# Layer 0 of a two-layer graph network on one core: products ahead of their sums, turned rows copied behind the products, columns read one iteration later

## The chip, the cores and the metric

The kernel runs on one core of a Trainium2 chip. A core has five engines that run side by side, each through its own list of instructions in order: TensorE (PE, matrix products, with a weight load PEld that overlaps them), VectorE (DVE), ScalarE (ACT), GpSimd (POOL) and SyncE (SP). They wait for each other on semaphores only. SP, ACT and POOL also start transfers (DMA), which 16 DMA engines carry out. The metric is the device time of one execution in microseconds (us); less is better. The kernel before takes 928.87 us, the median of 6 runs that lie between 926.46 and 931.57.

## The reference, cut to what matters

`x` has 3327 rows of 512 numbers, `adj` is a 0/1 matrix of 3327 x 3327, symmetric, with ones on its diagonal and about nine ones in a row. Layer 0 is graph attention with 4 heads of 128 numbers, then relu, the addition of the input and a normalisation of each row:

```python
feats = jnp.einsum('nf,hfo->hno', X, W)
e_s = jnp.einsum('hno,ho->hn', feats, a_self)
e_n = jnp.einsum('hno,ho->hn', feats, a_neigh)
logits = e_s[:, :, None] + e_n[:, None, :]
logits = jnp.where(logits > 0, logits, LRELU_ALPHA * logits)
logits = logits + NEG_INF * (1.0 - A)[None, :, :]
attn = jax.nn.softmax(logits, axis=-1)
out = jnp.einsum('hnm,hmo->hno', attn, feats) + b[:, None, :]
...
x = _layernorm(x + relu(out))
```

Layer 1 weighs the neighbours' new rows in a second way, adds a plain sum over neighbours, two gates, two projections and a second normalisation. It is not touched by the change, apart from its line numbers.

## The kernel before

**Sparse lists.** The kernel does not multiply by `adj`. A first stage (to about 207 us of the span) turns the matrix into a short list of neighbours for each row, computes `feats` and the two scores for all rows, and writes them as rows of 520 numbers to a table in device memory (`table0`). Rows are sorted by their number of neighbours into 26 tiles of 128 rows. `CAPS[j]` is the number of neighbours that tile j has room for (14 down to 5 in the first group of 12 tiles, 14 down to 4 in the second group of 14). The first tile of each group has a "stair" more, one slot in which longer lists share rows. The first group's sorted lists come through device memory; the second group's are sorted in place by `sort1` (two of its 14 tiles in each of the iterations 1 to 7), which lets TensorE place rows by a 0/1 matrix and ends with two VectorE copies out of PSUM into `srt[1]`. `climb` then works out the node ids of a stair (`ids2`).

**The stage in question** is the loop over `order0`, the 26 tiles of layer 0, from about 207 to 531 us of the span. For each tile:

- *Gather.* POOL issues one indirect transfer for each slot (`indirect`, L615): 128 rows of the table, picked by a column of the list, into a ring of 42 slots (`ring`). The first one of a tile brings two slots, the tile's own x and its own features. `plan` lays out all slots beforehand; `gather` issues what fits in the program's order. A gather into a slot waits, by semaphore, for the instructions that read the slot's former content, above all for the TensorE product 42 slots earlier. POOL has 254 gathers in layer 0, in order, and nothing between them; after the last one come 14 scatters (`put_rows`, L146), which write the second group's finished rows to `table1`.
- *Weights.* `weigh_a` and `weigh_b`: some eight short VectorE instructions and one ScalarE exponential give the attention weights of a tile. They read every slot of the tile, so they wait for its last gather. ScalarE also copies ids and the tile's own x out of the ring (L768, L771).
- *Sum.* `attend`: each slot's 512 numbers are multiplied by the weights, on VectorE (L797) or, for every third slot, on ScalarE in four pieces (L795). TensorE adds the slots up in PSUM by products with the identity (L803), one fp32 product being two matmul instructions. `attend` issues the products and sums of a tile slot by slot and, behind slot 2, calls `between`, which is `columns2` of the tile two places earlier. `lean` tiles add the bias on VectorE (L802) to slot 0 instead of by a product of their own (L789).
- *Finish.* `finish` (L885, VectorE: relu and the addition of x) waits for the sum; `norm.add` takes statistics and, at the ends of groups of 4, 4, 4, 4, 4, 3, 2 and 1 tiles, a reciprocal square root in 13 short instructions.
- *Columns.* The new row is needed in 8 small products for layer 1. `columns1` turns the row on TensorE (L822), `columns2a` copies it out of PSUM on ScalarE (L828), `columns2` multiplies (L834), `columns3` copies the 8 results on VectorE (L838).
- *Publish.* `publish` normalises a group's tiles (L842 on ScalarE, L845 and L846 on VectorE) and starts the write to `table1`, two iterations after the group's end.

Nothing reorders instructions: each engine works through them as the Python code issues them. Before, one iteration i of the loop issues in this order: publish; `columns2a` of tile i-2; `attend` of tile i with `columns2` of tile i-2 inside; `finish` of tile i-1 and further gathers; `columns1` and statistics of tile i-1; `columns3` of tile i-2; `sort1`; `climb` at i = 8; `weigh` of tile i+1. Tiles 0 and 1 are attended ahead of the loop. Places (0 to 25) are counted along `order0`.

Layer 1 gathers from `table1` through the same ring, so its first gather waits for the last write of layer 0.

Of the kernel before, what the change touches and what calls it, by code (L numbers as in the profile page):

```python
# [78 lines left out]
def sparse_pass(  # L79
# [463 lines left out]
    def sort1(to, t0, t1):  # L543


        n = NG[1]
        if t0 == 0:
            in_place.append(ps.tile([P, KT * P], F32, tag="pt", name="sorted1")[:, : n * W1])
        for t in range(t0, t1):
            row_is = ls.tile([P, P], F32, tag="row_is", name=f"row_is{t}", bufs=2)  # L550
            nc.vector.tensor_scalar(row_is, columns, to[:, 1, t : t + 1], None, ALU.is_equal)
            spread = ls.tile([P, n, W1], F32, tag="spread", name=f"spread{t}", bufs=2)
            nc.vector.scalar_tensor_tensor(
                spread, tiles_.to_broadcast([P, n, W1]), to[:, 0, t : t + 1],
                st1[:, t : t + 1, :].to_broadcast([P, n, W1]), ALU.is_equal, ALU.mult,
            )
            nc.tensor.matmul(
                in_place[0], row_is, spread.rearrange("p t w -> p (t w)"), start=(t == 0), stop=(t == n - 1)
            )
        if t1 == n:  # L560
            by_tile = in_place[0].rearrange("p (t w) -> p t w", t=n)
            nc.vector.tensor_copy(srt[1][:, :, : S + 2], by_tile[:, :, : S + 2])
            nc.vector.tensor_copy(srt[1][:, :, S + 2 : W1].bitcast(F32), by_tile[:, :, S + 2 :])
# [34 lines left out]
    def climb(g, pool, psum):  # L598

        of = pool.tile([P, B + H], F32, tag="of", name=f"of{g}")  # L600
        nc.vector.tensor_copy(of[:, :B], srt[g][:, 0, C0 + 1 : S + 1])
        nc.vector.tensor_copy(of[:, B:], srt[g][:, 0, S + 2 : S + 2 + H].bitcast(F32))
        nc.tensor.matmul(psum, to_row, of, start=True, stop=True)
        nc.vector.tensor_mul(of[:, :B], psum[:, :B], step_of)
        id_ = pool.tile([P, 1], F32, tag="id_", name=f"id_{g}")
        nc.vector.tensor_reduce(id_, of[:, :B], AX.X, ALU.add)
        nc.vector.tensor_copy(ids2[g], id_)
        nc.vector.tensor_copy(es2[g], psum[:, B:])
# [134 lines left out]
    def weigh_a(j):  # L743
# [6 lines left out]
        if j in T0:  # L750
            logit = m0.tile([P, H], F32, tag="logit", name=f"logit{j}")
            nc.vector.tensor_add(logit, stair[j][:, F : F + H], es2[g])
            small = psx.tile([P, B * H], F32, tag="pcol", name=f"to_nodes{j}", bufs=2)
# [19 lines left out]
    def weigh_b(j):  # L773
# [5 lines left out]
        if j in T0:  # L779
            small = psx.tile([P, B * H], F32, tag="pcol", name=f"to_rows{j}", bufs=2)  # L780
            ws2[j] = to_rows(m0, small, f"n{j}", w[:, C0 + 1 :, :])

    def attend(j, lean, between):


        w = ws[j]
        acc = accs[j] = ps.tile([P, F], F32, tag="acc", name=f"acc{j}", bufs=2)
        if not lean:
            nc.tensor.matmul(acc, ident, bias0, start=True, stop=False)  # L789
        for s0, n, buf, o in got[j]:  # L790
            for s in range(s0, s0 + n):
                gv = buf[:, o + s - s0, 0:F].rearrange("p (h o) -> p h o", h=H)
# [7 lines left out]
                row = buf[:, o + s - s0, 0:F]  # L800
                if lean and s == 0:
                    nc.vector.tensor_add(row, row, bias0)  # L802
                nc.tensor.matmul(  # L803
                    acc, ident, row, start=(lean and s == 0), stop=(s == CAPS[j] and j not in T0)
                )
                if s == 2:
                    between()
        if j in T0:
# [4 lines left out]
            nc.tensor.matmul(acc, to_node, stair[j][:, 0:F], start=False, stop=True)  # L813

# [76 lines left out]
    for i in range(len(chunks)):  # L893
# [13 lines left out]
        if i == NC0 + 2:  # L907
            climb(0, p0, psl.tile([P, CH], F32, tag="pc1", name="climb0")[:, : B + H])
# [29 lines left out]
    for j in order0[:2]:  # L938
        weigh_a(j)
        weigh_b(j)  # L940
    for j in order0[:2]:
        attend(j, False, lambda: None)
    weigh_a(order0[2])
    weigh_b(order0[2])
    for j in order0[:2]:
        finish(j)
    ready = [[], []]
    for i in range(NT + 3):
# [3 lines left out]
        third = order0[i - 2] if 2 <= i < NT + 2 else None  # L952
        if third is not None:
            columns2a(third)
        if 2 <= i < NT:
            attend(order0[i], i >= 3, lambda: third is None or columns2(third))
        elif third is not None:
            columns2(third)
        if 0 < i <= NT:
            j = order0[i - 1]  # L960
            y = row1(j)[:, 0:F]
            if i > 2:
                finish(j)
            if not waiting:
                put_rows()
            columns1(j)
            done = norm.add(i - 1, y)
            if done:
                k0, scale, shift = done
                ready[1] = [  # L970
                    (order0[k], scale[:, k - k0 : k - k0 + 1], shift[:, k - k0 : k - k0 + 1]) for k in range(k0, i)
                ]
        if i > NT:
            put_rows()
        if 2 <= i < NT + 2:
            columns3(order0[i - 2])
        if 0 < i <= 7:
            sort1(rankis[1], 2 * i - 2, 2 * i)
        if i == 8:
            climb(1, m0, psx.tile([P, B * H], F32, tag="pcol", name="climb1", bufs=2)[:, : B + H])  # L980
# [10 lines left out]
        if 2 <= i < NT - 1:  # L991
            weigh_a(order0[i + 1])
            weigh_b(order0[i + 1])
# [658 lines left out]
```

## Time and profile before

One execution was profiled. It took 932.01 us, of which its span on the core is 930.1 us; 1.9 us lie around the span. It is 3.1 us above the median of the 6 runs.

| stretch of the span, us | PE busy, us | DVE busy, us | ACT busy, us | POOL busy, us |
|---|---|---|---|---|
| 207 to 245 (38) | 29.14 | 24.80 | 13.99 | 29.74 |
| 245 to 290 (45) | 45.00 | 35.04 | 17.95 | 34.64 |
| 290 to 340 (50) | 41.72 | 34.61 | 20.82 | 38.11 |
| 340 to 390 (50) | 43.90 | 42.45 | 24.39 | 38.42 |
| 390 to 440 (50) | 48.34 | 39.84 | 26.38 | 37.12 |
| 440 to 490 (50) | 48.80 | 41.44 | 26.19 | 37.99 |
| 490 to 530 (40) | 33.16 | 32.68 | 17.97 | 25.23 |

How to read it: busy time is the time in which an engine executes. The short step between two instructions in which it takes up the next one is not counted, nor is a wait. Matmul ends are modelled, so a PE that is busy throughout need not be at its peak. On the timeline of one engine each line has the start, the duration, the instruction with what it writes and reads, how often it is repeated, and in brackets the idle time before it with the event that ended it.

### The profile page before, as it was taken

What the parts mean: (1) busy time and instruction counts of PE and PEld (TensorE: products, weight loads), DVE (VectorE), ACT (ScalarE), POOL (GpSimd) and SP (SyncE); (2) the same over time, 40 slices, a digit from 0 to 9 for tenths busy, and PEclk for the clock granted to TensorE, in tenths of its full rate; (3) what the DMA queues carried; (4) which work ended last, traced back from release to release, by engine and by line L of the source; (5) the groups of instructions that cost most, each with busy time, mean ns of one, the idle gap of its engine ahead of it and who ended that gap; (6) DMA issues with size and microseconds to landing.
All of it is one profiled execution on the core that took longest, in us unless ns stands there. A gap on an engine that the chain in (4) does not pass through costs nothing. (4 is left out here: it accounts for less than half of the span.)

```text
span 930.1 us, 10307 instructions
## 1 busy us (share of the span) xinstructions
PE 784.7 (84%) x2518; PEld 413.7 (44%) x2518; DVE 734.5 (79%) x2100; ACT 288.1 (31%) x820; POOL 604.0 (65%) x641
## 2 busy tenths in 40 slices
PE   4698987327999889799998749999989999999893
PEld 3476775112455444344444414444444444444341
DVE  4387888884978668869887748799989989999973
ACT  0121221003355434445554312323231232322331
POOL 6710152757877777777777477777777777777611
PEclk9898998557899989799999859999999999999997
DMA  9999899999678788797777367777777777776401
GB/s 334 370 380 394 339 340 383 381 360 412 202 228 267 233 233 266 233 347 232 218 233 229 126 188 192 199 193 191 193 193 191 186 195 192 195 190 193 156 35 38
DMA packets 73349, 224.68 MB, mean 242 GB/s; under 512 B 12736, under 2 KB 16784, under 8 KB 72384
## 3 DMA queue, kind: packets, MB, share of 16 engines
q0 software_dynamic: 46368, 153.69, 55.4%
q1 hardware_dynamic: 24256, 68.13, 19.4%
q10 hardware_dynamic: 2656, 2.10, 0.7%
q8 instruction: 23, 0.38, 0.2%
q14 instruction: 46, 0.38, 0.1%
HBM read 203.02 MB, written 31.51 MB: 252 GB/s over the span
## 5 line engine op out<-in xcount | busy, mean ns | idle before, releaser
L615 POOL DMA_INDIRECT ring<-table,srt x464 | 485.0, 1045 | 158.7 <-issue 56.4
L803 PE MATMUL acc<-ring,ident 128*128 128x512 f32 x504 | 241.1, 623 | 21.7 <-DVE ring L802 15.0
L1097 DVE SCALAR_TENSOR_TENSOR sw<-ring,e,sw 128x512 f32<-128x512 f32 x226 | 169.3, 749 | 11.7 <-ACT sw L1081 7.5
L803 PEld LDWEIGHTS acc<-ring,ident 128*128 128x128 f32 x504 | 95.2, 198 | 134.2 <-issue 75.1
L1118 PE MATMUL acc<-ring,ident 128*128 128x512 f32 x264 | 126.6, 609 | 19.3 <-DMA ring<-table,srt 9.7
L371 PE MATMUL pf<-w,xc 128*128 128x260 f32 x416 | 105.0, 416 | 13.3 <-DVE w L311 13.3
L797 DVE TENSOR_TENSOR ring<-ring,w 128x512 f32<-128x512 f32 x176 | 111.8, 693 | 0.6
L371 PEld LDWEIGHTS pf<-w,xc 128*128 128x128 f32 x416 | 85.6, 208 | 30.1 <-DVE w L311 14.0
L1137 PE MATMUL po<-wsa,sT 128*128 128x512 f32 x208 | 95.0, 600 | 0.3 <-ACT sT L1130 0.3
L1137 PE MATMUL po<-wg,sT 128*128 128x512 f32 x208 | 93.7, 593 | 0.0
L795 ACT ACTIVATE ring<-ring,w 128x128 f32<-128x128 f32 x304 | 91.5, 390 | 0.0
L1118 PEld LDWEIGHTS acc<-ring,ident 128*128 128x128 f32 x264 | 49.9, 194 | 89.7 <-issue 45.4
L383 POOL DMA_DIRECT2D table<-row x26 | 14.3, 549 | 84.0 <-ACT st L380 81.6
L1099 DVE TENSOR_TENSOR ring<-ring 128x512 f32<-128x512 f32 x94 | 65.0, 692 | 3.2
L1169 ACT ACTIVATE za<-za 128x512 f32<-128x512 f32 x26 | 16.4, 632 | 151.5 <-DVE za L1167 151.5
L1137 PEld LDWEIGHTS po<-wsa,sT 128*128 128x128 f32 x208 | 40.2, 194 | 51.2 <-issue 48.7
L1137 PEld LDWEIGHTS po<-wg,sT 128*128 128x128 f32 x208 | 39.4, 190 | 48.8 <-issue 47.8
L402 PE MATMUL pc<-at,pow 128*32 128x512 bf16 (+1 forms) x182 | 23.5, 414 | 34.2 <-DMA at<-in_adjB 23.5
L762 ACT ACTIVATE w<-w 128x40 f32<-128x40 f32 (+10 forms) x26 | 6.2, 238 | 131.9 <-DVE w L761 131.9
L375 ACT COPY row<-pf 128x512 f32<-128x512 f32 x26 | 15.2, 586 | 97.0 <-PE pf L371 51.4
L1130 ACT COPY sT<-pt 128x512 f32<-128x512 f32 x52 | 28.4, 587 | 39.0 <-PE pt L1128 39.0
L834 PEld LDWEIGHTS pcol<-v,xt 128*128 128x128 f32 x208 | 28.8, 202 | 14.6 <-issue 12.2
(254 smaller groups left out, 938.3 us busy)
## 6 DMA issues: line engine op xcount, KB each, us to landing
at<-in_adjB SPq DMA_DIRECT2D x78, 512.0 KB, 11.6
ring<-table,srt POOLq DMA_INDIRECT x464, 3.9
table<-row POOLq DMA_DIRECT2D x26, 260.0 KB, 6.1
xc<-in_xB SPq DMA_DIRECT2D x6, 1024.0 KB, 8.6
own<-in_xo SPq DMA_DIRECT2D x1, 3640.0 KB, 45.2
own<-table SPq DMA_DIRECT2D x1, 3640.0 KB, 55.3
at<-in_adjL SPq DMA_DIRECT2D x13, 256.0 KB, 10.5
table<-in_xo SPq DMA_DIRECT2D x1, 3120.0 KB, 28.9
```

What stands on the lines that cost most here:

```text
L371: nc.tensor.matmul(pf[:, hh, :HC], xc[:, k, o : o + P], w0[:, k, hh, :], start=(k == 0), stop=(k == KT - 1))
L402: nc.tensor.matmul(pc[32 * c : 32 * c + 32, : nt * P], pow2[:, s, :], loaded[i, m], start=(s == 0), stop=(m + 1 not in ms or s == 3),)
L615: return nc.gpsimd.indirect_dma_start(out=out_, out_offset=None, in_=table, in_offset=bass.IndirectOffsetOnAxis(ap=ap, axis=0)).ins
L795: nc.scalar.activation(gv[:, h, :], gv[:, h, :], AF.Copy, scale=w[:, s, h : h + 1])
L797: nc.vector.tensor_tensor(gv, gv, w[:, s, :].rearrange("p (h o) -> p h o", o=1).to_broadcast([P, H, FO]), ALU.mult)
L803: nc.tensor.matmul(acc, ident, row, start=(lean and s == 0), stop=(s == CAPS[j] and j not in T0))
L834: nc.tensor.matmul(pcol, xt1[:, k, :], v1[:, k, :], start=(k == 0), stop=(k == KT - 1))
L1097: nc.vector.scalar_tensor_tensor(sw, g[:, i, 0:F], e[:, s : s + 1], sw, ALU.mult, ALU.add)
L1099: nc.vector.tensor_add(g[:, i, 0:F], g[:, i - 1, 0:F], g[:, i, 0:F])
L1118: nc.tensor.matmul(plain[j], to, row, start=(not sums_of_two and i == 0), stop=(sums_of_two and i == len(rows) - 1),)
L1130: nc.scalar.copy(sT, pt)
L1137: nc.tensor.matmul(proj[j], sT[:, k, :], wt[:, k, :], start=(half + k == 0), stop=(half + k == KT))
```

## The change

The function `attend` is split in two. `multiply` issues all multiplications of a tile (the same instructions on VectorE and ScalarE), `add_up` then all its TensorE sums; the call in the middle is gone. `climb` and the end of `sort1` are split off (`climb_a`, `climb_b`, `sorted1`). The loop starts at tile 0 with only `weigh` of tile 0 ahead of it, has one iteration more at its end, and issues in another order:

```diff
-    norm = Norm(...)
-    for j in order0[:2]:
-        weigh_a(j)
-        weigh_b(j)
-    for j in order0[:2]:
-        attend(j, False, lambda: None)
-    weigh_a(order0[2])
-    weigh_b(order0[2])
-    for j in order0[:2]:
-        finish(j)
+    weigh(at_(0))
     ready = [[], []]
-    for i in range(NT + 3):
-        for args in ready[0]:
-            publish(*args)
-        ready = [ready[1], []]
-        third = order0[i - 2] if 2 <= i < NT + 2 else None
-        if third is not None:
-            columns2a(third)
-        if 2 <= i < NT:
-            attend(order0[i], i >= 3, lambda: third is None or columns2(third))
...
+    for i in range(NT + 4):
+        cur, nxt, done, turned_ = at_(i), at_(i + 1), at_(i - 1), at_(i - 2)
+        past = [at_(k) for k in ([i - 3] if i < NT else [i - 2]) if at_(k) is not None]
+        if i == NT:
+            past = [at_(i - 3)] + past
+        if cur is not None:
+            multiply(cur, i >= 3)
+        if cur is not None:
+            add_up(cur, i >= 3)
+        if done is not None:
+            finish(done)
+            columns1(done)
+            if not waiting:
+                put_rows()
+            norm_done = norm.add(i - 1, row1(done)[:, 0:F])
+        if nxt is not None:
+            weigh(nxt)
+        if turned_ is not None:
+            columns2a(turned_)
+            columns2(turned_)
+        for j in past:
+            columns3(j)
+        for args in ready[0]:
+            publish(*args)
+        ready = [ready[1], []]
+        if i > NT:
+            put_rows()
...
+        if i < 7:
+            sort1(rankis[1], 2 * i, 2 * i + 2)
+        if i == 7:
+            sorted1()
         if i == 8:
-            climb(1, m0, ...)
+            climb_a(1, m0)
+        if i == 9:
+            climb_b(1, m0)
...
-        if 2 <= i < NT - 1:
-            weigh_a(order0[i + 1])
-            weigh_b(order0[i + 1])
```

The new function for the sums:

```diff
+    def add_up(j, lean):
+
+        acc = accs[j] = ps.tile([P, F], F32, tag="acc", name=f"acc{j}", bufs=2)
+        rows = [] if lean else [(ident, bias0)]
+        rows += [(ident, buf[:, o + k, 0:F]) for _, n, buf, o in got[j] for k in range(n)]
+        if j in T0:
+            rows.append((to_node, stair[j][:, 0:F]))
+        for k, (to, row) in enumerate(rows):
+            nc.tensor.matmul(acc, to, row, start=(k == 0), stop=(k == len(rows) - 1))
```

So, within an iteration: ScalarE multiplies tile i before it copies turned rows, and these are of tile i-2, turned an iteration ago; `columns2` of tile i-2 stands on TensorE behind the whole sum of tile i and the turn of tile i-1; `columns3` reads tile i-3; `publish` stands near the end of the iteration, after `weigh` of tile i+1, instead of at its start; `sort1` starts at iteration 0 and its result is copied out at iteration 7. Small products that used the PSUM tag `pcol` (stairs, `climb`) get a buffer of their own (`aux`). The instructions on each engine are the same in kind and number, and POOL's list is the same gathers and scatters in the same order.

## The prediction

> **What bounds the kernel now.** I read the busy time by stretches first (the table above). In 390 to 490 us TensorE is busy 97% of the time, POOL only 75%, so TensorE looks like the bound of layer 0. The groups of instructions say something else:
>
> ```profile
> L615 POOL DMA_INDIRECT ring<-table,srt x464 | 485.0, 1045 | 158.7 <-issue 56.4
> L803 PE MATMUL acc<-ring,ident 128*128 128x512 f32 x504 | 241.1, 623 | 21.7 <-DVE ring L802 15.0
> ```
>
> A gather (L615) takes about 0.95 us and is followed by a short pause. The POOL timeline shows what that pause is:
>
> ```profile
> 236.16 7.61 POOL L615 DMA_INDIRECT ring<-table,srt  x1 [0.30 <-issue]
> 244.07 1.32 POOL L615 DMA_INDIRECT ring<-table,srt  x1 [0.30 <-issue]
> ...
> 403.23 0.95 POOL L615 DMA_INDIRECT ring<-table,srt  x1 [0.30 <-issue]
> 404.72 0.95 POOL L615 DMA_INDIRECT ring<-table,srt  x1 [0.55 <-PE acc L803]
> 406.84 0.96 POOL L615 DMA_INDIRECT ring<-table,srt  x1 [1.17 <-DMA ring<-own,srt]
> 408.11 0.95 POOL L615 DMA_INDIRECT ring<-table,srt  x1 [0.30 <-issue]
> ...
> 503.91 0.95 POOL L615 DMA_INDIRECT ring<-table,srt  x1 [0.30 <-issue]
> 505.16 1.43 POOL L146 DMA_INDIRECT table<-x1b,srt  x1 [0.30 <-issue]
> ...
> 528.80 0.98 POOL L146 DMA_INDIRECT table<-x1b,srt  x1 [7.85 <-DVE x1b L846]
> 530.09 0.98 POOL L146 DMA_INDIRECT table<-x1b,srt  x1 [0.31 <-issue]
> 531.38 0.98 POOL L146 DMA_INDIRECT table<-x1b,srt  x1 [0.30 <-issue]
> 534.94 0.99 POOL L615 DMA_INDIRECT ring<-table,srt  x1 [2.57 <-PE acc L1118]
> ```
>
> The 0.30 us stands before almost every gather, whatever it is put down to: it is the cost of taking up the next one. So gathers follow each other every 1.25 us at best (408.11 to 503.91 holds 75 steps of 1.28 on average). Between 244 and 505 us POOL waits for anything once, for about 1.1 us at 404 to 407.
>
> Could POOL be held by ring slots that TensorE frees late? I laid out the slots from `CAPS` and the plan, and for each gather took the product 42 slots earlier. Example: the gather at 393.07 fills slot 184; slot 142 is row 3 of place 13, the first of 12 products (24 matmuls) that run from 387.15 for 10.55 us, so it ended at 387.15 + 10.55/12 = 388.03, 5.0 us before. Over all gathers this lead is 2.1 us at its smallest (at 224.51), never under 5 us from 393 on, 25 us for the last tile. POOL never waits for a slot: **the gather stream is the bound of layer 0**. TensorE's 97% is a queue that works off 0.86 us a slot against POOL's 1.25.
>
> Towards the end the others have caught up and wait for landings (VectorE, then TensorE timeline):
>
> ```profile
> 488.75 0.23 DVE L749 TENSOR_TENSOR w<-ring,srt 128x40 f32<-128x40 f32 x1 [2.44 <-DMA ring<-table,srt]
> ...
> 502.28 0.20 DVE L749 TENSOR_TENSOR w<-ring,srt 128x40 f32<-128x40 f32 x1 [2.12 <-DMA ring<-table,srt]
> ...
> 523.36 0.69 DVE L885 SCALAR_TENSOR_TENSOR x1b<-acc,x1b 128x512 f32<-128x512 f32 x1 [1.47 <-PE acc L803]
> ```
>
> ```profile
> 491.19 0.60 PE L822 MATMUL x1t<-ident,x1b 128*128 128x128 f32 x4
> 492.24 2.84 PE L803 MATMUL acc<-ring,ident 128*128 128x512 f32 x6 [0.44 <-DVE ring L802]
> ...
> 505.74 4.54 PE L803 MATMUL acc<-ring,ident 128*128 128x512 f32 x6 [3.32 <-DVE ring L802]
> ...
> 519.52 1.12 PE L803 MATMUL acc<-ring,ident 128*128 128x512 f32 x2 [0.18 <-ACT ring L795]
> ```
>
> Place 24's weights start at 502.28, when its last gather lands; from there to 534.94, the first gather of layer 1, the way leads over VectorE and TensorE. This tail is where the order of instructions can tell.
>
> **The change, part by part.** *Waits of TensorE on ScalarE.* The copy of turned rows stood ahead of ScalarE's multiplications and waited for TensorE's turn behind the whole last sum. Now it reads a turn one iteration old, behind the multiplications. That removes some 15 waits of 0.18 us (as at 519.52), 2.7 us. *The list's end.* VectorE waited 6.3 us at 312 for the last `sort1` product, TensorE then 4.0; `climb` cost VectorE 4.8 and TensorE 4.2 at 330 to 339. Split off, both go. *columns3* no longer waits for a product inside the next sum: 13.2 us of VectorE waits in all. All of this lies between 230 and 475 us under the gather stream, with a lead of 2 us or more: worth **0**. It makes TensorE idle longer, not the stage shorter. Were the cover gone (POOL as fast as TensorE), these TensorE waits would be worth 2.7 + 4.0 + 4.2, about 11 us.
>
> *POOL's list* is unchanged, and the first tiles free slots no later. `sort1` now puts two products, about 2 us of TensorE, between sums 0 and 1; but sum 0 starts some 1.9 us earlier, as VectorE multiplies tile 0 (at 212.2) before it weighs tile 1. Sum 1 starts near 223 either way, and the 2.1 us lead stands. The late consumers of the list are not late: `srt[1]` is read by POOL at 329, its copies come before 318; `ids2` at 357.93, with `climb_b` some 10 us ahead. SP's queue holds the first group's writes and two weight loads (at 394), which move back by up to one iteration; layer 1 first uses them after 555 us.
>
> *The 1.1 us at 404* stands while these two loads fill the DMA queues (DMA share 0.97 to 1.04 in 395 to 410). The loads move a few us, the collision stays: bounds 0 and -1.1, I take **0**, by the DMA rows.
>
> *The tail.* VectorE from 502.28 in the new order, each piece by its length in the old trace: weights of place 24 1.99; `columns3` 0.15; multiplications 4.94; finish and statistics of 23 1.63; weights of 25 1.71; 0.15; multiplications of 25 3.13; finish, statistics and root of 24 4.39; 0.15; publish of places 20 to 22, now here, 1.20. Sum 19.44: VectorE reaches the last finish at 521.7. TensorE: sum 24 starts at 505.9 and takes ten slots of 0.86; turn 0.43 and `columns2` 0.81 of older tiles; five slots: 505.9 + 8.6 + 1.24 + 4.3 = 520.0 if it has run until then, 522.0 with a slow start like that of 505.74 (six matmuls in 4.54 us against 2.74 elsewhere). The old order had one `columns2` more ahead of the last finish. So the last finish starts between 521.7 and 522.2 instead of 523.36. From it to the last scatter the same chain follows (528.80 - 523.36 = 5.44, and 0.25 for two more `columns3` ahead): gain 0.9 to 1.4 us, I take **-1.1**. The three scatters of places 20 to 22 now start near 521, not 516, and are done by 525, before the next three at about 527.5. Upstream there is one tight spot: publish of places 16 to 19 (1.60) moves behind the weights of place 23, and eats 1.75 of the 2.12 us that VectorE waits at 502.28. Were it late there by 1 us, the gain would be gone.
>
> The TensorE clock gate is the rule that speaks against the change. The trace has the row above: after 3.32 us of idling the first three slots took 1.8 us longer, and the granted clock is 0.50 to 0.57 between 200 and 220 us, where it does little. The Trainium skill, TensorE: Matmul & The Clock Gate, "What's actually happening", says that the array falls to half its clock after an idle window of about 3.4 us and needs as long a busy one to recover. By the row one slow start in the tail costs 0 to 0.5 us of the end, as above; by the page a halved clock for a whole window would cost an estimated 1.7 us, and the gain would be a loss of about 0.6.
>
> **Sum.** 932.01 (profiled: 930.1 and 1.9 around it) - 1.1 = 930.9 for an execution like the profiled one, which lies 3.1 above the median; on the median 928.87 - 1.1 = **927.8 us**. 0.3%, about what a measurement can tell from no change, is 2.8 us.
>
> **The rivals.**
>
> *A gather stream that stalls more (slower).* At 236.16 one gather took 7.61 us, 6.66 over the usual 0.95. It waited for no slot, and no byte moved in 240 to 244 us; VectorE ran almost without a gap then. If such a hold comes from VectorE's unbroken work, the change, which takes VectorE's waits away, may bring one more, and one decides: 927.8 + 6.7 = 934.5. For it: the unexplained row. Against it: it is one of 482, and the unbroken run from 248.75 to 253.79 has four gathers of 0.95. The Trainium skill, SBUF — State Buffer, "Who interferes with whom", says that VectorE copies and casts in a two-port mode lock GpSimd out of writing descriptors, while `tensor_tensor`, as it infers, does not; here the products are `tensor_tensor`, and the row at 248.75 agrees.
>
> *That hold goes away (faster).* Were 236.16 an ordinary gather, POOL would be 6.66 ahead, less what the lead of 2.6 to 3.9 us at 244 to 250 holds back after TensorE's own gain of about 2 us there: 4.7 more, 923.1.
>
> *TensorE is the bound after all (faster).* Then the 11 us above and the tail's 3.3 us wait come off: near 914. For it: 97% busy. Against it: every lead.
>
> *It doesn't do what it says.* If ScalarE's copy waited all the same, everything above would still be hidden: 928.9.
>
> **How the numbers follow.** Chances: my forecast 0.60 (927.8, own range 926 to 930), hidden and nothing in the tail 0.09, one more stall 0.16, the stall gone 0.11, TensorE 0.04. The range leaves out TensorE and part of the stalled cases: 922.5 to 932.5. Faster: 0.11 + 0.04 and 0.09 from the forecast's lower edge, 0.24. Slower: 0.16 and 0.03 from its upper edge, 0.19. Same: 0.57.
>
> **What would show it.** Right: gathers still about 1.28 us apart, the last near 504; the 0.18 us waits, the one at 312 and those of `columns3` gone; TensorE idle longer before 490; last scatter near 530. Wrong: POOL waits for TensorE between 244 and 504, another gather of several us, or a last scatter after 532.

## The result, and the profile after

The changed kernel takes 931.05 us (median of 35 runs, 926.10 to 936.09), the kernel before in the same comparison 928.57 (78 runs, 923.59 to 934.63): 1.0023 of before, 95% interval 1.0012 to 1.0035. By this ratio that is 2.1 us slower (1.1 to 3.25), where 1.1 us faster was forecast. The time lies in the forecast's range, on the other side of no change.

The profiled execution of the changed kernel took 929.29 us (span 927.6), 1.8 below its median; that of the kernel before 932.01, 3.4 above its own. The two profiles therefore show a gain where the medians show a loss, and neither total can be read from them; only pieces that repeat can. The groups of instructions, changed kernel (busy us, mean ns of one, idle time before them and what ended most of it):

```profile
L625 POOL DMA_INDIRECT ring<-table,srt x464 | 481.7, 1038 | 156.4 <-issue 65.3
L823 PE MATMUL acc<-ring,ident 128*128 128x512 f32 x504 | 233.5, 620 | 4.8 <-DVE ring L808 3.3
```

TensorE's idling ahead of the sums fell from 21.7 to 4.8 us: the waits that the change was to remove are gone. A gather takes as long on average as before (1038 ns against 1045). POOL's timeline, changed kernel (start, length, tile, idle before and what ended it):

```profile
219.25 4.35 POOL L625 DMA_INDIRECT ring<-table,srt  x1 [0.30 <-PE acc L823]
223.91 0.95 POOL L625 DMA_INDIRECT ring<-table,srt  x1 [0.30 <-PE acc L823]
...
236.66 0.95 POOL L625 DMA_INDIRECT ring<-table,srt  x1 [0.30 <-PE sorted L557]
237.91 0.95 POOL L625 DMA_INDIRECT ring<-table,srt  x1 [0.30 <-issue]
...
402.45 1.26 POOL L625 DMA_INDIRECT ring<-table,srt  x1 [1.37 <-PE acc L823]
...
500.24 0.95 POOL L625 DMA_INDIRECT ring<-table,srt  x1 [0.30 <-issue]
501.50 1.34 POOL L146 DMA_INDIRECT table<-x1b,srt  x1 [0.30 <-issue]
...
525.09 1.27 POOL L146 DMA_INDIRECT table<-x1b,srt  x1 [4.03 <-DVE shifted L853]
526.66 0.99 POOL L146 DMA_INDIRECT table<-x1b,srt  x1 [0.30 <-issue]
527.95 0.98 POOL L146 DMA_INDIRECT table<-x1b,srt  x1 [0.30 <-issue]
531.74 0.99 POOL L625 DMA_INDIRECT ring<-table,srt  x1 [2.80 <-issue]
```

Two things are new. A gather at 219 takes 4.35 us, where the profile of the kernel before has none of that kind so early; the 7.61 us one at 236 is missing in this execution (it turns out to be there in nearly all others). And between the last finish and layer 1's first gather (531.74) something takes longer, which VectorE and TensorE show:

```profile
498.47 0.20 DVE L759 TENSOR_TENSOR w<-ring,srt 128x40 f32<-128x40 f32 x1 [0.81 <-DMA ring<-table,srt]
...
517.45 0.68 DVE L893 SCALAR_TENSOR_TENSOR x1b<-acc,x1b 128x512 f32<-128x512 f32 x1
...
521.50 0.16 DVE L718 SCALAR_TENSOR_TENSOR rdn<-mvn,rrn 128x1 f32<-128x1 f32 x1
521.58 0.23 DVE L846 COPY x1b<-pcol 128x8 f32<-128x8 f32 x2
523.77 0.17 DVE L846 COPY x1b<-pcol 128x8 f32<-128x8 f32 x1 [1.96 <-PE pcol L842]
```

```profile
518.68 0.96 PE L842 MATMUL pcol<-v,xt 128*128 128x8 f32 x8
521.89 1.85 PE L842 MATMUL pcol<-v,xt 128*128 128x8 f32 x8 [2.25 <-DVE x1b L846]
```

Place 24's weights start at 498.47 and the last finish at 517.45: 18.98 us, against a forecast of 19.44. But TensorE's last `columns2` (place 25) stands until 521.89, although its turn had been copied by 519.5: both `pcol` buffers (the PSUM tiles for the 8 columns) hold columns of places 23 and 24, and the `columns3` that empties one (521.58) is in VectorE's order behind finish, statistics and the whole root of place 25. The last `columns3` then waits 1.96 us, and `publish`, which frees the last three scatters, behind it. From the last finish to the first of these scatters: 7.64 us, before 5.44; to layer 1's first gather 14.29, before 11.58.

Five of the nine comparisons below ran where the gathers of every kernel, old and new, were held again and again by something that these runs do not show ("held" below; kernel before 1067 to 1075 us), so only their ratios and the pieces of their profiles that repeat are used; the other four ("undisturbed") had the kernel before at 927.4 to 929.6 us.

### The profile page after: what moved, and what is told of

It is laid out like the page before. It is cut to its first block, busy times and chain, and to the rows that moved or that the text cites. A ratio compares the mean times of both kernels' runs of the same rounds, so it can differ in the third digit from the quotient of the medians.

```text
span 927.6 us, 10309 instructions
## 1 busy us (share of the span) xinstructions
PE 781.9 (84%) x2518; PEld 415.1 (45%) x2518; DVE 733.9 (79%) x2100; ACT 286.6 (31%) x820; POOL 600.2 (65%) x641
## 5 line engine op out<-in xcount | busy, mean ns | idle before, releaser
L625 POOL DMA_INDIRECT ring<-table,srt x464 | 481.7, 1038 | 156.4 <-issue 65.3
L823 PE MATMUL acc<-ring,ident 128*128 128x512 f32 x504 | 233.5, 620 | 4.8 <-DVE ring L808 3.3
L823 PEld LDWEIGHTS acc<-ring,ident 128*128 128x128 f32 x504 | 98.5, 199 | 124.4 <-issue 86.2
L1129 PE MATMUL acc<-ring,ident 128*128 128x512 f32 x264 | 127.7, 613 | 20.7 <-DMA ring<-table,srt 10.6
L371 PE MATMUL pf<-w,xc 128*128 128x260 f32 x416 | 102.7, 409 | 13.1 <-DVE w L311 13.1
L1129 PEld LDWEIGHTS acc<-ring,ident 128*128 128x128 f32 x264 | 49.9, 194 | 91.3 <-issue 45.1
L383 POOL DMA_DIRECT2D table<-row x26 | 14.3, 550 | 87.3 <-ACT st L380 84.6
L842 PE MATMUL pcol<-v,xt 128*128 128x8 f32 x208 | 28.4, 263 | 11.8 <-ACT xt L836 9.6
```

Of the source, the lines that this page charges most:

```text
L371: nc.tensor.matmul(pf[:, hh, :HC], xc[:, k, o : o + P], w0[:, k, hh, :], start=(k == 0), stop=(k == KT - 1))
L625: return nc.gpsimd.indirect_dma_start(out=out_, out_offset=None, in_=table, in_offset=bass.IndirectOffsetOnAxis(ap=ap, axis=0)).ins
L823: nc.tensor.matmul(acc, to, row, start=(k == 0), stop=(k == len(rows) - 1))
L842: nc.tensor.matmul(pcol, xt1[:, k, :], v1[:, k, :], start=(k == 0), stop=(k == KT - 1))
L1129: nc.tensor.matmul(plain[j], to, row, start=(not sums_of_two and i == 0), stop=(sums_of_two and i == len(rows) - 1),)
```

## The experiments

Three theories stood at first: A, the tail's wait for a `pcol` buffer; B, the gather stream is held more; C, layer 1. The long gathers of all profiles then turned B into H: VectorE's unbroken run of products holds a gather.

### The two kernels again

Unchanged copies of both, for more profiles.

> The changed kernel as it is, a second profile. Theory A (all of it is the tail: the last columns2 finds no free pcol buffer): 1.002 of the kernel before; from place 24's weights to the last scatter some 29.5 us, against 29.10 in the profile of before, and from the first gather of an own row to the first scatter no longer than before's 304 us. Theory B (the gather stream is held more): the same ratio, but that stretch is longer than before's by some 1.5 us, in gathers of several us near 219 or 236 us, or in waits for TensorE. Theory C (what is left over is layer 1): from the first gather of layer 1 to the end 396 us or more, against 395.2.

> The kernel before as it is, a second profile: ratio 1.000, within 0.0015. It says how much the pieces of one kernel differ from one profiled execution to the next: the stretch from the first own gather to the first scatter (303.9 us so far), the gathers of over 3 us in it (one, 7.61 us), the tail (29.10 us), layer 1 (395.2 us). If the tail repeats within 0.3 us and the stream varies by some us, then a piece of a single profile is evidence for the tail only.

> The changed kernel once more, since the first comparison ran where every gather stream was held for 100 us and more and so says nothing of 2 us. Theory A (the tail): 1.002 of before; last finish to the first of the last three scatters 7.6 us as in both its profiles so far, against 5.4 in both of before; own gather to first scatter 299 to 304 us. Theory B (the stream): that stretch longer than 304 us, by holds of some us in gathers between 200 and 250 us. Theory C: layer 1 of 396 us or more, against 395.2.

> The kernel before once more. What this profile is to tell: the way from place 24's weights to the last finish was 21.08 us in its first profile, with TensorE's slow start (six matmuls in 4.54 us after 3.32 us of idling), and 19.39 us in its second, without. Theory A in its full form (the slow start that the change was credited with taking away isn't there in most executions of the kernel before, so that the pcol wait alone is left): about 19.4 to 20 us here, and last finish to first gather of layer 1 11.6 us again. If the slow start belongs to every undisturbed execution: 21 us, and the tail explains only 0.4 to 0.6 us of the 2.1 us loss. Where the gather stream is held: first own gather of the own rows to the last gather of layer 0 some 210 us or more, against 198 to 201 us in the seven profiles of the new order.

> The changed kernel once more, now that a comparison has run undisturbed (928.86 us for the kernel before). Both theories: 1.002 of before. Theory A: from place 24's weights to the last finish 19.0 to 19.8 us and from there to layer 1's first gather 14.3 us, 33.3 to 34.1 together. Theory B: the stretch from the first gather after the own rows' table to the last gather of layer 0 longer than in before_again3 by 1.5 us or more.

> The kernel before, undisturbed if the chip stays so: ratio 1.000. If TensorE's slow start in the tail is an accident of its first profile: place 24's weights to the last finish 19.4 to 20 us, so that the tail is 2.2 to 2.7 us shorter than the changed kernel's and explains the whole loss. If it belongs to the kernel: 21 us again, and the tail explains 0.4 to 0.9 us.

Measured, all with held streams: changed kernel 0.9918 (0.983 to 1.0007), 0.982 (0.971 to 0.993) and 0.980 (0.968 to 0.992) of before; the copies of before 1.006, 0.994 (0.989 to 0.9997) and 1.003. The kernel before thus differs from itself by half a per cent here. None gave 1.002: where gathers are held in this way, the new order is 1 to 2% faster in these three. Such a hold, in the first copy of the changed kernel: VectorE's timeline, and the GB/s row of the DMA view of 314 to 328 us (40 slices of 0.35 us):

```profile
319.87 0.17 DVE L846 COPY x1a<-pcol 128x8 f32<-128x8 f32 x1 [2.32 <-PE acc L823]
322.71 0.28 DVE L551 TENSOR_SCALAR row_is<-columns,to 128x128 f32<-128x128 f32 x1 [2.68 <-remote]
```

```profile
GB/s 380 345 357 285 297 273 178 178 238 273 166 178 214 214 202 250 262 190 190 273 202 95 238 297 48 12 0 0 0 0 0 95 119 285 226 143 71 119 261 357
```

Nothing moves for five slices, and VectorE stands too. After such a hold POOL waits for sums of TensorE, up to 6 us: the cover that the prediction put over TensorE's waits is gone there. That the waits which the change removes are what makes the new order faster then fits, but no run takes it apart. From the first gather of an `own` row to the last gather of layer 0 the old order took 213.9, 206.5 and 204.4 us, the new one 197.2 to 201.0 in eleven profiles.

The end of the tail repeats to 0.03 us in the four profiles of each kernel. Last finish to layer 1's first gather: old order 11.58, 11.59, 11.58, 11.58; changed kernel 14.29, 14.32, 14.31, 14.30. The way ahead of it does not settle as well: from place 24's weights to the last finish the copies of before took 19.39, 24.95 and 22.25 us, held, so they do not tell whether TensorE's slow start at 505.74 (21.08 us in all) belongs to the kernel. C is not needed: layer 1 took 395.2 us in the profile of before, 395.9 in that of the changed kernel, and 394.2 to 395.4 in the four undisturbed profiles below, with no order among old and new.

### columns3 of place 23 ahead of the last root

```diff
-        if i == NT:
-            past = [at_(i - 3)] + past
...
             columns1(done)
+            if i == NT:
+                columns3(at_(i - 3))
```

> The changed kernel with columns3 of place 23 right after the last finish, ahead of the last statistics and root, so that a pcol buffer is free when place 25's turn has been copied. Theory A: the 1.96 us wait of the last columns3 goes and the last scatter comes 1.6 to 2.0 us earlier after place 24's weights (some 27.6 us), the whole 0.998 of the changed kernel, 1.000 of the kernel before. Theory B: the same 1.6 to 2.0 us off, if the rest of the loss lies in the stream; then 1.0003 of before and the rest still to be found. If something else sets the last scatters (POOL's own pace, ScalarE's publish): 1.0023 as it was.

> The changed kernel with columns3 of place 23 right after the last finish. In the first, disturbed comparison the way from the last finish to the first of the last three scatters was 5.51 us instead of 7.63, so the edit does what it is meant to. Theory A: the whole becomes 1.000 of before (0.9995 to 1.0005), 2 us less than the changed kernel. Theory B: the same 2 us, with the stream's part left over: 1.0003 to 1.001. If layer 1 took the gain back (its first gathers waiting for something else): 1.002.

> The changed kernel with columns3 of place 23 right after the last finish. Theory A: 2.1 us less than the changed kernel (last finish to layer 1's first gather 12.2 us instead of 14.3), so 1.000 of before. Theory B: the same 2.1 us, if B's loss comes on top of the tail: 1.0005 or more of before. If layer 1 takes it back: 1.002.

Measured, all held: 0.9908 (0.979 to 1.003), 0.989 (0.980 to 0.998), 0.990 (0.982 to 0.997), which does not tell it from the changed kernel. The piece does: last finish to layer 1's first gather 12.19, 12.22 and 12.72 us instead of 14.3. POOL's timeline in the first of them, whose last finish started at 604.47:

```profile
609.98 1.27 POOL L146 DMA_INDIRECT table<-x1b,srt  x1 [1.91 <-DVE shifted L853]
611.56 0.98 POOL L146 DMA_INDIRECT table<-x1b,srt  x1 [0.30 <-issue]
612.85 0.98 POOL L146 DMA_INDIRECT table<-x1b,srt  x1 [0.30 <-issue]
616.66 0.98 POOL L625 DMA_INDIRECT ring<-table,srt  x1 [2.83 <-issue]
```

5.51 us to the first scatter, and the last `columns2` follows without a wait. The occupied buffer costs the tail 1.6 to 2.1 us.

### Places 23 and 24 wholly ahead of the last root

```diff
         if i == NT:
-            past = [at_(i - 3)] + past
+            past = []
...
             columns1(done)
+            if i == NT:
+                columns3(at_(i - 3))
+                columns2a(turned_)
+                columns2(turned_)
+                columns3(turned_)
+                for args in ready[0] + ready[1]:
+                    publish(*args)
+                ready = [[], []]
             if not waiting:
                 put_rows()
...
-        if turned_ is not None:
+        if turned_ is not None and i != NT:
```

> The changed kernel with, after the last finish, columns3 of place 23, columns2 and columns3 of place 24 and the publishing and scatters of both ahead of the last statistics and root, so that two of the last three scatters run while VectorE works out the last root. Theory A: the scatter of place 25 starts some 3.1 us earlier than in the changed kernel (a root put off by 1 us, no wait for columns2, one scatter left instead of three): 928 or 0.999 of before. If the last scatters do not set the start of layer 1: 1.002.

> The changed kernel with columns of places 23 and 24, their publishing and scatters ahead of the last statistics and root, once more. In its first profile the last finish to the first gather of layer 1 took 11.67 us, against 14.3 us in the changed kernel and 11.6 us in the kernel before. Theory A: 2.6 us less than the changed kernel, 0.9995 of before, if the gather stream isn't held, since its way from place 24's weights to the last finish is that of the changed kernel (19.0 to 19.8 us). Theory B (the stream brings a loss of its own): 1.0005 to 1.001 of before. With a held stream, as in the three comparisons so far: 0.98 to 0.99 of before.

> The changed kernel with columns of places 23 and 24, their publishing and scatters ahead of the last statistics and root; 0.9999 of before in its first undisturbed comparison (0.9976 to 1.0023). Theory A: 2.6 us less than the changed kernel, 0.9995 of before. Theory B: 1.0005 or more.

Measured: held 0.982 (0.974 to 0.990) and 0.988 (0.980 to 0.996). Undisturbed (the second) 927.63 us, 0.9999 of before (0.9976 to 1.0023): by the middle value the loss is gone, 2.2 us by the ratios, but with some 2.4 of uncertainty. The piece is clear: in its profile the last finish lies 11.40 us ahead of layer 1's first gather, 2.9 less than in the changed kernel. Two scatters now run under the root. The same profile has two long gathers; POOL's timeline:

```profile
217.23 0.94 POOL L625 DMA_INDIRECT ring<-table,srt  x1 [0.30 <-issue]
218.48 4.03 POOL L625 DMA_INDIRECT ring<-table,srt  x1 [0.30 <-DMA ring<-table,srt]
...
236.65 6.88 POOL L625 DMA_INDIRECT ring<-table,srt  x1 [0.30 <-issue]
```

and VectorE's beside the first:

```profile
218.03 0.65 DVE L553 SCALAR_TENSOR_TENSOR spread<-tiles__359,to,st 128x420 f32<-128x420 f32 x1
218.60 3.09 DVE L804 TENSOR_TENSOR ring<-ring,w 128x512 f32<-128x512 f32 x5
222.10 0.69 DVE L893 SCALAR_TENSOR_TENSOR x1a<-acc,x1a 128x512 f32<-128x512 f32 x1 [0.41 <-PE acc L823]
```

The gather ends at 222.51, VectorE's five products at 221.69: 0.82 us apart. In the changed kernel's own profile it is 223.60 and 222.78 (five products from 219.69, 3.09 us), again 0.82. For the 7.61 us gather of the kernel before it is 243.77 against 242.95, again 0.82; VectorE's timeline there:

```profile
236.25 6.10 DVE L797 TENSOR_TENSOR ring<-ring,w 128x512 f32<-128x512 f32 x10
242.27 0.68 DVE L810 TENSOR_TENSOR ring<-ring,w_n 128x512 f32<-128x512 f32 x1
242.87 0.68 DVE L692 BATCH_NORM_STATS2 st<-x1a 128x6 f32<-128x512 f32 x1
```

An ordinary gather lasts 0.95, so a held one does its last 0.82 us once the run of products is over. VectorE itself need not stop for that: here the statistics follow without a gap. VectorE starts the next independent product before the last one is through (every 0.60 us, each 0.68 long); a run has no gap. That is H. The gathers are counted from 0 in order of issue: 39 to 41 fall beside tile 1's products, 51 or 52 beside tile 2's. Of ten profiles of the new order with `sort1` in its changed place and unbroken products, nine have the first hold (3.1 to 4.35 us) and nine the second (6.9 to 8.0). Not every gather in a run is held: in the changed kernel's profile the ten products of tile 2 run from 235.45, and the gathers at 236.66 and 237.91 shown above take 0.95.

All gathers of layer 0 together, from gather 26 on in all twenty profiles (4560), say what kind of instruction it is. The 451 that take over 1.05 us all begin while VectorE executes an instruction that reads two operands from SBUF (on-chip memory): a product, a bias addition, a `spread` of `sort1` or one of the last steps of the lists. The 1321 that begin while VectorE executes nothing take at most 0.98 us, and the 342 that begin beside a `finish`, which is as long as a product but reads one operand from PSUM, at most 0.95.

They also say in part which gathers pass. Of 659 that begin within 0.05 us of a product's start, 653 take under 1.0 us, and the product beside each takes 0.72 us or more instead of 0.68; so it is at 236.66 and 237.91. And most are held for one product only: 87 that begin inside a product with two or more products behind it take 1.31 to 1.48 us and end 0.81 to 0.84 us after that one product, while the run goes on. Why a few beside tiles 1 and 2 are held to the end of the run stays open.

### sort1 back in its old place; sort1 ahead of the weights

The first puts the products one iteration later, their end at the last of them:

```diff
-        if i < 7:
-            sort1(rankis[1], 2 * i, 2 * i + 2)
+        if 0 < i <= 7:
+            sort1(rankis[1], 2 * i - 2, 2 * i)
```

> The changed kernel with the sort1 products one iteration later, as in the kernel before, and their end in the iteration of the last one; climb stays split. Theory B in the form that the products between sums 0 and 1 hold the first ring slots back: 1.0005 to 1.001 of before, the first own gather to the first scatter shorter by 1.5 us or more than in the changed kernel. Theory A: 1.002 as the changed kernel, with the 6 us wait of VectorE for the last sort1 product back and hidden.

> The changed kernel with the sort1 products one iteration later, as in the kernel before, and their end in the iteration of the last one. Theory B, that the products between sums 0 and 1 free the first ring slots late: 1.0005 to 1.001 of before, and the gathers between 215 and 245 us no longer wait for TensorE's sums. Theory A: 1.002, as the changed kernel.

The second leaves the iteration and moves the same two lines from the end of it to just ahead of `weigh(nxt)`:

> The changed kernel with one thing moved: the sort1 products stand ahead of the next tile's weights instead of ahead of its products, so that the weights' short dependent instructions lie between them and the products. Theory H: the gathers 38 to 42 take 5.5 to 6 us instead of 8.1 to 8.4 (a hold shorter than 2 us is left, where a gather starts in the five products alone), so 928 us, 0.9990 to 0.9995 of before, with the tail's 14.3 us from the last finish to layer 1's first gather unchanged. If the place of sort1 doesn't matter: 8 us for gathers 38 to 42 and 1.002 of before.

Measured, all held: 0.988 (0.976 to 1.0005), 0.983 (0.976 to 0.990), and 1067.67 us against 1067.96 (no interval), so the totals tell nothing. In none of the three is gather 39, 40 or 41 held, where seven of the eight other held profiles of the new order have 3.1 to 3.5 us there. The old order, held, has 3.38 us there in three of three; only its one undisturbed profile with unbroken products has none, so that this hold is new rests on one profile. The way from gather 38 to 42 was 7.20, 6.95 and 7.02 us in the three (5.5 to 6 expected for the last), 9.21 in the changed kernel. With `sort1` ahead of the weights the gather beside tile 2 still took 4.44 us: the products' run alone can hold one.

### VectorE's runs broken, in both orders

The same lines in `attend` of the kernel before and in `multiply` of the changed one; the copy of one column waits for its product and leaves a gap of 0.04 us. A product then comes every 0.79 us instead of every 0.60:

```diff
                 if lean and s == 0:
                     nc.vector.tensor_add(row, row, bias0)
+                if not lean and s % 3 != 2:
+                    nc.vector.tensor_copy(gap, row[:, 0:1])
```

> The kernel before with a copy of one column behind each of VectorE's products in the first three tiles (nothing else). Theory H: the gathers 51 to 53, 9.15 us in its profile and 8.8 to 9.4 in the three disturbed ones, take 2.5 to 4.5 us, no gather lasts over 2 us, and 4 to 6.6 us of it show in the whole: 922.5 to 925 us, 0.9930 to 0.9955 of before. If a long gather comes from elsewhere: 9 us again and 1.000. If the time comes back as waits for ring slots: holds gone, and 0.999 or more.

> The changed kernel with a copy of one column behind each of VectorE's products in the first three tiles, and nothing else: the same edit as before_breaks made in the old order. Theory H (in the new order slots come free earlier, so a hold isn't hidden behind waits for slots): gathers 38 to 42 in 5.5 to 6.5 us, 51 to 53 in 3 to 5 us, no gather over 2 us, and 4 to 6 us of it in the whole, 925 to 927 us, 0.996 to 0.998 of before, with the tail's 14.3 us from the last finish to layer 1's first gather unchanged. If the holds are worth nothing here either, as in the old order: 1.002, and the whole of the loss is the tail.

Measured, both undisturbed: old order 927.60 us, 0.9996 (0.9977 to 1.0015); new order 927.25 us, 0.9968 (0.9946 to 0.9990). The edit is worth nothing in the old order and 5.1 us (2.8 to 7.4, from both intervals) in the new one. POOL's timeline, old order with breaks, then new order with breaks:

```profile
236.74 1.79 POOL L615 DMA_INDIRECT ring<-table,srt  x1 [0.30 <-issue]
238.84 1.27 POOL L615 DMA_INDIRECT ring<-table,srt  x1 [0.30 <-ACT ring L796]
242.29 0.97 POOL L615 DMA_INDIRECT ring<-table,srt  x1 [2.18 <-PE acc L806]
244.00 0.94 POOL L615 DMA_INDIRECT ring<-table,srt  x1 [0.75 <-DVE ring L798]
245.75 0.94 POOL L615 DMA_INDIRECT ring<-table,srt  x1 [0.81 <-DVE ring L813]
```

```profile
236.77 1.08 POOL L625 DMA_INDIRECT ring<-table,srt  x1 [0.30 <-DVE gap L811]
238.15 1.27 POOL L625 DMA_INDIRECT ring<-table,srt  x1 [0.31 <-ACT ring L803]
240.29 0.95 POOL L625 DMA_INDIRECT ring<-table,srt  x1 [0.87 <-DVE ring L805]
242.01 1.39 POOL L625 DMA_INDIRECT ring<-table,srt  x1 [0.77 <-DVE gap L811]
```

The 7 us hold is gone in both. In the old order POOL then waits for ring slots (2.18, 0.75, 0.81, and 1.50 at 229), the third outcome of the expectation: part of the hold had been hidden by them. In the new order with breaks the slots come free earlier (the first slot of tile 2 is summed 35.9 us after gather 26, in the old order with breaks 38.8), so less of a hold is hidden. Part only: in the old order's two profiles gathers 51 to 58 still take 3.5 us less with breaks (12.84 against 16.30), and why the medians show nothing of that stays open. In the new order two things missed the expectation: one gather takes 2.02 us, and the end of the tail 13.65 us instead of 14.3. The old order's tail without a long TensorE stall shows as well; TensorE's timeline, old order with breaks:

```profile
503.45 2.84 PE L806 MATMUL acc<-ring,ident 128*128 128x512 f32 x6 [0.19 <-DVE ring L803]
```

Six matmuls in 2.84 us, not the 4.54 of 505.74 in the first profile: 19.38 us from place 24's weights to the last finish, not 21.08; it is one profile, of a kernel with the breaks.

### Both mended

Tail as in the second tail edit, `sort1` ahead of the weights, products broken.

> after_ahead (the changed kernel with its tail put right) and, in the first three tiles, a copy of one column behind each of VectorE's products, which waits for that product and so breaks VectorE's unbroken run, and the sort1 products ahead of the next tile's weights instead of ahead of its products. Theory H (a gather that starts in an unbroken run of VectorE is held until the run ends, plus 0.82 us): no gather of layer 0 lasts over 2 us; where the gather stream isn't held from elsewhere, 3 us less for the hold beside tile 1 and 4 to 6 us less for the one beside tile 2, so 919 to 923 us, 0.990 to 0.994 of before. If the long gathers come from something else (the copies of own rows on the other queue, the place in the list): gathers 39 to 41 and 51 to 53 still last 3 to 8 us, and 0.9995 of before.

Measured: 922.09 us, 0.9933 of before (0.9906 to 0.9961), faster than both kernels; no gather of layer 0 over 1.5 us. The six undisturbed profiles by stretches, us (gather 26 is the first that reads the finished table):

| | before | before, broken | changed | changed, broken | changed, tail mended | both mended |
|---|---|---|---|---|---|---|
| gather 38 to 42 | 5.45 | 5.65 | 8.41 | 5.72 | 8.10 | 5.60 |
| gather 51 to 53 | 9.15 | 5.55 | 2.50 | 3.52 | 8.48 | 4.06 |
| gather 26 to the last of layer 0 | 302.68 | 299.16 | 298.16 | 296.48 | 302.06 | 296.96 |
| last gather to last finish | 19.45 | 18.06 | 17.21 | 17.51 | 16.89 | 17.07 |
| last finish to layer 1's first gather | 11.58 | 11.58 | 14.29 | 13.65 | 11.40 | 11.38 |
| sum of the last three | 333.71 | 328.80 | 329.66 | 327.64 | 330.35 | 325.41 |

Each is one execution; the profile of the changed kernel is the one without the second hold, worth some 6 us in row two.

## Why the prediction was wrong, by its steps

*The bound and TensorE's waits.* Right: gathers 1.29 us apart (402.45 to 500.24), all the named waits gone, TensorE idle later instead (busy 43.35 of the 50 us from 440 to 490, before 48.80), nothing of it seen in the total. "POOL never waits for a slot" was a little too strong: in the profile of before the gather at 227.41 stands 0.70 us, not 0.30, behind a sum of TensorE. The 11 us put on the waits "were the cover gone" fit the held streams, where the new order gained 0.8 to 2.0% of some 1070 us, 9 to 21 us, in its three unchanged copies; the variant with `sort1` ahead of the weights gained nothing there (1067.67 against 1067.96).

*"POOL's list is unchanged ... the 2.1 us lead stands."* The first step that failed. The lead stood (no new slot wait), but the length of a gather did not: the step looked at when slots come free and not at what VectorE does beside the gather. The new order puts `sort1`'s VectorE work and tile 1's products in one run at 218 us, and a gather there is held by 3 us (row one: 8.1 and 8.4 against 5.45 in the one profile of the old order). It also frees tile 2's slots earlier, which the step valued at nothing too: with all runs broken the stream is 2.7 us shorter in the new order (299.16 and 296.48). With both holds in, that gain is gone (302.06 with the tail mended, 302.68 in the kernel before). With the runs broken in both orders, the change measures 0.9968 / 0.9996, 2.6 us faster (with some 2.7 of uncertainty): the forecast's side. So the unbroken runs cost the change some 4.7 us (1.8 to 7.6), by the middle value enough for its loss alone.

*The rival of a stream that stalls more* named this mechanism, VectorE's unbroken run, and its price, "one more" hold. It was put at 0.16 because four gathers of 0.95 us lay in another such run. That row was read too strongly: a run lets some gathers pass and holds another, and the gather just ahead of the four, at 248.21, took 1.45 us. The rival that the hold at 236.16 goes away for 4.7 us fell: in the old order its going is worth nothing in the whole (0.9996, at most 2.1 us); slot waits take a part of its place, and the rest is not explained.

*The tail.* Its VectorE sum was right (19.44 against 18.98). Two things were not. "From it to the last scatter the same chain follows" failed: the chain now holds `columns3` of place 23 behind the root and so the last `columns2` for want of a `pcol` buffer: 2.2 us to the first of the last scatters (7.64 against 5.44), and 2.7 in all to layer 1's first gather. The reader of the diff could have counted buffers: two, and three places' columns alive at once in the last iterations. And the gain ahead of it, 1.1 to 1.7 us, came mostly from a slow start of TensorE (505.74) that the other undisturbed profile of that order, the one with breaks, lacks. The tail from the last gather to layer 1 was 31.50 and 31.16 us in the new order, 31.03 and 29.64 in the old: 0.1 to 1.9 us lost where 1.1 was to be won.

*The collision at 404* stayed (1.37 us), as taken.

The two failed steps are shown each by itself: mending the tail takes 2.9 us off the end of the tail and gives 0.9999 (0.9976 to 1.0023), breaking the runs alone gives 0.9968 (0.9946 to 0.9990), both give 0.9933 (0.9906 to 0.9961). How the 2.1 us divide between them is not settled better than these intervals; `sort1`'s place alone was tried only under held streams.

*The clock gate*, which the prediction named as what speaks against the change, did act in the new tail, behind the wait for the buffer. In the eight profiles with the changed kernel's end of the tail, TensorE idles for 2.07 to 2.25 us ahead of its last `columns2`. In five of them (the changed kernel, its three copies and one with `sort1` back) the granted clock is then 0.50 to 0.52, `columns2` takes 1.80 to 1.85 us, and the way from the last finish to layer 1's first gather is 14.3 to 14.4. In the other three the clock is 0.81 to 1.00, `columns2` takes 1.03 to 1.18, and the way is 13.55 to 13.65. So the slow clock costs some 0.7 us of the 2.7, above the 0 to 0.5 that the prediction took from its row, and without it some 2.0 are left to the buffer. The idle window of about 3.4 us in the rule that the prediction cites from the Trainium skill, TensorE: Matmul & The Clock Gate, "What's actually happening", is longer than any of these waits; here the clock fell after less.

*The Trainium skill, SBUF — State Buffer, "Who interferes with whom"* was used for half of what it says. It infers that `tensor_tensor` leaves descriptor writing alone, but states beside it that a VectorE instruction with two inputs in SBUF contends with a GpSimd instruction that reads SBUF, and that this is an exclusive lock. The same page says under "SBUF: two separate sides" that whichever of the two starts first has it for the whole instruction. A gather takes its 128 indices from SBUF (`srt`). That all 451 lengthened gathers begin beside such an instruction agrees with the first of these, and the 653 that go first and the 87 held for one product agree with the last. The 25 of over 3 us do not: they are held over several products.

## What to carry to other kernels

Where POOL's gathers set the pace, look at what VectorE does beside each of them: an instruction that reads two operands from SBUF can hold one, and a run of them without a gap sometimes does so for its whole length. A tiny dependent instruction behind each breaks the run, at 0.19 us a product here. Whether a removed stall pays depends on the wait behind it, so take it away in both orders before crediting it. When a read moves an iteration later, count the buffers that are then alive at once, in the last iterations above all.

## What the runs showed of the hardware

A gather of over 3 us in layer 0 always ends with VectorE's products: of 25 in the fourteen profiles of both orders and the tail edits, 22 end 0.82 us after the last product of a run and three 0.96 us, whether they lasted 3.1 or 8.0 us. The shorter holds add up as well: the gathers of under 3 us lose 6 to 11 us in all over layer 0 in each of the twenty profiles, counted above 0.95 us a gather. And in the held executions no byte moved for some 2 us at a time, 25 to 30 us apart (POOL resumes at 323, 352, 380 and 405 us in the copy shown), with VectorE standing too (2.68 us): the kernel of 929 us took 1070, though its first gather came at 163 us as in the others (162 to 164 us where nothing was held). What stops them stays open.
